# Small VectorE steps of the norms and of a feed-forward layer written as scalar_tensor_tensor in a two-layer hybrid transformer kernel

## The chip, the cores and the metric

The kernel runs on one core of a Trainium2 chip. The metric is the device time of one execution in microseconds (us). Of the kernel before there are three runs: 2148.95, 2151.29 and 2156.46 us, median 2151.29 us. One more execution, 2155.31 us long, was taken with the hardware profiler; all views of the profile below are of that one.

## The reference

The input `x` has 4 sequences of 512 rows and 256 columns, in float32. Eight sublayers follow each other, each on a layer-normalised copy of `x` that is added back:

```python
x = x + mla(layernorm(x))            # low-rank-key attention, 16 heads
x = x + ffn(layernorm(x))            # the feed-forward layer of this change
x = x + cosine_attention(layernorm(x))
x = x + ffn(layernorm(x))            # the same weights again
x = x + gated_linear_attention(layernorm(x))
x = x + workspace(layernorm(x))      # 16 slots a sequence, two rounds
x = x + lora_attention(layernorm(x))
x = x + workspace(layernorm(x))
```

The parts that the change touches are the norms and the feed-forward layer (`eps` is 1e-7 in the latter):

```python
def layernorm(x):  m, v = mean(x), var(x);  return (x - m) / sqrt(v + 1e-5)

def ffn(x):
    out = (x @ weight) * scale
    v_norm = maximum(norm(out), eps)                 # one number a row
    out = out * (tanh(v_norm) / (v_norm + eps))
    o_norm = maximum(norm(out), eps)
    return out * minimum(0.99 / o_norm, 1.0)
```

Row norms of the same kind (a value to the power -1/2) occur in all four attention and workspace layers too.

## The kernel before

A sequence is held in SBUF as 4 tiles of 128 rows by 256 columns (`self.x[b]`, shape 128 x 4 x 256). The four sequences are worked through one after another inside each sublayer, and sublayers overlap: the feed-forward layer of a sequence is a Python generator (`ffn_steps`) whose pieces are called from the loops of the attention layer before or after it (the dictionaries `woven` and `extra`).

By time in the profile the stages are roughly: low-rank attention 0 to 615 us, cosine attention 615 to 1345 us, gated linear attention 1345 to 1580 us, workspace 1580 to 1720 us, LoRA attention 1720 to 2030 us, workspace again to the end.

The order of TensorE's instructions is that of the program text (`tc.manual_schedule(engines={PE})`). The order on VectorE, ScalarE and GpSimd is not written out: a planner makes it when the program is built. It plays the program through with its own costs for each instruction and, whenever an engine is free, takes the ready instruction that ranks first. On the chip each engine then runs its list strictly in that order, and an instruction that has to wait holds up all that stand behind it on its engine.

The lines that matter here:

- `rpow` (line 149) computes `(mul*in + eps)^(-1/2)`. VectorE makes `a = in*mul + eps` (L154, one `tensor_scalar`), ScalarE makes `exp(-0.5*ln(a))` (L155, L156), and VectorE refines it by one Newton step: `t = a*out` (L157, `tensor_tensor`), `t = t*(-0.5)*out` (L158) and `out = (t+1.5)*out` (L160, or L163 into a wide tile), the last two as `scalar_tensor_tensor`. It is called by `moments` for a layer norm (128 x 4 values, mul 1.0, eps 1e-5), by `ffn_steps` (128 x 4, mul 1.0, eps 0.0), by the entry of the workspace layer (128 x 16, mul 1.0, eps 1e-6), and elsewhere with other `mul`: by the query norms of cosine attention (tile `crn`, 128 x 512, in from PSUM), its keys (`crk`), the low-rank keys (`kvrs`) and three norms inside the workspace (`ws_rms`, `ws_ms`, `ws_r`).
- `rpow_aside` is the same on GpSimd and is not touched.
- `ffn_steps` (line 481): after the matmul, `fy = py*scale` (L497, VectorE), four squares with row sums on ScalarE (L500), and then a chain of small steps on 128 x 4 values: a floor (L503), `rpow`, `n*ss` (L505), a floor (L507), tanh on ScalarE (L509) with a change of ScalarE's function table before it and one after it (L510, recorded as L170), `v+eps` (L511), a reciprocal (L512), products and a floor (L513 to L515), a reciprocal (L516), `min(0.99*n, 1)` (L517), a product (L518), and four updates of `x` (L520, already `scalar_tensor_tensor`, 128 x 256).
- GpSimd's larger instructions are the additions of exponentials in cosine attention (L687, 128 x 1024), the scaling of probabilities in low-rank attention (L402), products in gated linear attention (L893, L930 to L933), masks (L1541), rope sums (L1476, L1477) and memsets (L1405 to L1415).

Of the kernel before, what the change touches and what calls it, by code (L numbers as in the profile page):

```python
# [13 lines left out]
ALU = mybir.AluOpType  # L14
# [6 lines left out]
NI = T // P  # L21
# [4 lines left out]
class Model:  # L26
# [122 lines left out]
    def rpow(self, out, in_, mul, eps, tmp, wide=None):  # L149


        nc = self.nc
        a, t = tmp
        nc.vector.tensor_scalar(a, in_, mul, eps, op0=ALU.mult, op1=ALU.add)  # L154
        nc.scalar.activation(out, a, AF.Ln)  # L155
        nc.scalar.activation(out, out, AF.Exp, scale=-0.5)  # L156
        nc.vector.tensor_tensor(t, a, out, op=ALU.mult)  # L157
        nc.vector.scalar_tensor_tensor(t, t, -0.5, out, op0=ALU.mult, op1=ALU.mult)  # L158
        if wide is None:
            nc.vector.scalar_tensor_tensor(out, t, 1.5, out, op0=ALU.add, op1=ALU.mult)  # L160
        else:
            t, r = (v.unsqueeze(len(v.shape)).to_broadcast(wide.shape) for v in (t, out))
            nc.vector.scalar_tensor_tensor(wide, t, 1.5, r, op0=ALU.add, op1=ALU.mult)  # L163

    def tmps(self):
        return [self.small.tile([P, NI], F32, name=f"rp{k}", tag=f"rp{k}") for k in range(2)]
# [314 lines left out]
    def ffn_steps(self, b, pause=True):  # L481
        nc = self.nc
        w, s = self.ffn_w, self.ffn_s
        eps = 1e-7
        xn, xt = self.norm_tiles()
        self.layernorm(xn, self.x[b])
        p2 = self.norm
        if pause:
            yield
        self.turned(xn, xt)  # L490
        yield
        py = self.two().rearrange("p a (i d) -> p (a i) d", d=D)
        for i in range(NI):
            self.mm(py[:, i, :], [(xt[:, c, i * P : (i + 1) * P], w[:, c, :]) for c in range(NC)])
        y = p2.tile([P, NI, D], F32, name="fy", tag="fy")
        ss = self.small.tile([P, NI], F32, name="f_ss", tag="f_ss")
        nc.vector.tensor_tensor(y, py, s.unsqueeze(1).to_broadcast([P, NI, D]), op=ALU.mult)  # L497
        for i in range(NI):
            sq = p2.tile([P, D], F32, name="fsq", tag="fsq")
            nc.scalar.activation(sq, y[:, i, :], AF.Square, accum_out=ss[:, i : i + 1])  # L500

        n = self.small.tile([P, NI], F32, name="f_n", tag="f_n")
        nc.vector.tensor_scalar_max(ss, ss, 1e-30)  # L503
        self.rpow(n, ss, 1.0, 0.0, self.tmps())
        nc.vector.tensor_tensor(n, n, ss, op=ALU.mult)  # L505
        v = self.small.tile([P, NI], F32, name="f_v", tag="f_v")
        nc.vector.tensor_scalar_max(v, n, eps)  # L507
        f = self.small.tile([P, NI], F32, name="f_f", tag="f_f")
        nc.scalar.activation(f, v, AF.Tanh)  # L509
        self.logs()  # L510
        nc.vector.tensor_scalar_add(v, v, eps)  # L511
        nc.vector.reciprocal(v, v)  # L512
        nc.vector.tensor_tensor(f, f, v, op=ALU.mult)  # L513
        nc.vector.tensor_tensor(n, n, f, op=ALU.mult)
        nc.vector.tensor_scalar_max(n, n, eps)  # L515
        nc.vector.reciprocal(n, n)  # L516
        nc.vector.tensor_scalar(n, n, 0.99, 1.0, op0=ALU.mult, op1=ALU.min)  # L517
        nc.vector.tensor_tensor(f, f, n, op=ALU.mult)  # L518
        for i in range(NI):
            nc.vector.scalar_tensor_tensor(  # L520
                self.x[b][:, i, :], y[:, i, :], f[:, i : i + 1], self.x[b][:, i, :], op0=ALU.mult, op1=ALU.add
            )
        yield
# [1314 lines left out]
```

## Time and profile before

| what | value |
|---|---|
| median of three runs | 2151.29 us |
| the profiled execution, whole | 2155.31 us |
| its span, first to last instruction | 2153.5 us |
| VectorE busy | 1268.0 us, 3185 instructions |
| GpSimd busy | 577.8 us, 530 instructions |
| TensorE's mean granted clock | 0.971 |

The 1.8 us between the whole execution and its span lie ahead of the first instruction and behind the last. "Busy" counts an instruction from its recorded start to its recorded end, so that an instruction that has started, but is held up, counts as busy. The names in a line of the profile are those of the tiles, `out<-in`; `DVE` is VectorE, `PE` TensorE, `ACT` ScalarE, `POOL` GpSimd, and `L503` is line 503 of the kernel before.

### The profile page before, as it was taken

To read this page: it belongs to the slowest core of one execution; us is meant where nothing else is said; L and a number is where in the kernel's file an instruction comes from. 1 tells how busy PE (TensorE), PEld (TensorE's weight loads), DVE (VectorE), ACT (ScalarE), POOL (GpSimd) and SP (SyncE) were. 2 spreads that over 40 slices of the span, in tenths; PEclk is the share of its full clock that TensorE was granted. 3 is DMA by queue.
4 is the path that set the end of the run, shared out by engine and by line. 5 is a ranking of instruction groups with operands and counts; after the bars stand their busy time and mean duration, and the time that the engine had idled before them with its cause. 6 is when DMAs were issued, how large, how long until landed. Compare 5 with 4: busy or idle time off the path is not lost.

```text
span 2153.5 us, 25620 instructions
## 1 busy us (share of the span) xinstructions
PE 1988.9 (92%) x9414; PEld 1062.3 (49%) x9414; DVE 1268.0 (59%) x3185; ACT 761.1 (35%) x1696; POOL 577.8 (27%) x530
## 2 busy tenths in 40 slices
PE   7999999999899999999999999988988989899886
PEld 4546555564454454544454454523355644444454
DVE  5565655656446434653664454398955766656545
ACT  2433443434323222322232223234224334334542
POOL 2433333433302212212212221156720122212100
PEclk9999999999999999999999999988899999999898
DMA  5020000000000000000000000010000000000001
GB/s 177 1 91 1 1 1 1 1 1 1 20 1 0 0 1 0 0 1 0 0 1 0 1 0 0 1 46 0 1 25 1 1 1 1 1 1 1 1 1 40
DMA packets 19837, 22.87 MB, mean 11 GB/s; under 512 B 4832, under 2 KB 17664, under 8 KB 19328
## 3 DMA queue, kind: packets, MB, share of 16 engines
q1 hardware_dynamic: 19712, 21.24, 3.0%
q8 instruction: 74, 1.21, 0.2%
q14 instruction: 51, 0.42, 0.1%
HBM read 19.14 MB, written 2.10 MB: 10 GB/s over the span
## 4 chain that ended last, share of the span: by engine, by line
PE 62%; DVE 16%; issue 11%; ACT 6%; POOL 4%; DMA 1%; SPq 0%; POOLq 0%; DVEq 0%; ACTq 0%
PE ps_two L238 26%; PE ps_acc L238 11%; PE ps_two L390 5%; PE ps_acc L429 3%; PE ps_two L1508 3%; DVE ps_two L256 3%; PE ps_two L417 2%; POOL e L687 2%; PE ps_two L1551 2%; DVE gs L888 2%; PE ps_acc L1249 1%; PE ps_two L654 1%; DVE ln_st L178 1%; ACT prob L397 1%; PE ps_acc L645 1%
## 5 line engine op out<-in xcount | busy, mean ns | idle before, releaser
L687 POOL TENSOR_TENSOR e<-e 128x1024 f32<-128x1024 f32 x64 | 150.7, 2355 | 619.4 <-ACT e L679 592.2
L256 DVE CUSTOM_DVE_ANT_0 ps_two<-ps_two,mask 128x256 f32<-128x256 f32 (+3 forms) x512 | 249.7, 503 | 74.3 <-PE ps_two L390 40.7
L679 ACT ACTIVATE e<-ps_two 128x1024 f32<-128x1024 f32 x128 | 130.8, 1023 | 346.8 <-PE ps_two L238 346.6
L238 PE MATMUL ps_acc<-e,cv 128*128 128x512 f32 x512 | 234.9, 601 | 1.4 <-DVE cot L685 0.9
L402 POOL TENSOR_TENSOR prob<-prob,psum_row 128x256 f32<-128x256 f32 (+3 forms) x128 | 159.7, 1255 | 284.6 <-DVE psum_row L401 278.4
L238 PE MATMUL ps_two<-cq,ckt 128*128 128x512 f32 x512 | 230.5, 593 | 3.0 <-DVE cq L656 3.0
L397 ACT ACTIVATE prob<-ps_two,nmax 128x128 f32<-128x128 f32 (+3 forms) x256 | 132.5, 526 | 148.6 <-DVE nmax L256 139.4
L238 PEld LDWEIGHTS ps_acc<-e,cv 128*128 128x128 f32 x512 | 93.5, 190 | 138.3 <-issue 116.0
L238 PEld LDWEIGHTS ps_two<-cq,ckt 128*128 128x128 f32 x512 | 96.6, 190 | 116.9 <-issue 114.8
L238 PE MATMUL ps_two<-own_xt,s 128*128 128x512 f32 x200 | 108.7, 675 | 13.9 <-DVE prt L129 11.1
L238 PE MATMUL ps_two<-own_xt,s16a 128*128 128x512 f32 x256 | 114.9, 592 | 0.1
L238 PE MATMUL ps_two<-s16b,cot 128*128 128x256 f32 x512 | 113.1, 379 | 0.0
L1540 ACT ACTIVATE lo_ex<-ps_two 128x1024 f32<-128x1024 f32 (+3 forms) x128 | 85.3, 704 | 72.8 <-PE ps_two L1508 67.5
L390 PE MATMUL ps_two<-kvt,qx 64*128 64x256 f32 (+3 forms) x512 | 103.6, 481 | 6.1 <-ACT qx L378 2.4
L417 PEld LDWEIGHTS ps_two<-ident,prob 128*128 128x128 f32 x640 | 71.0, 142 | 74.6 <-issue 48.5
L417 PE MATMUL ps_two<-ident,prob 128*128 128x128 f32 x640 | 94.6, 279 | 14.0 <-ACT qx L378 4.5
L238 PEld LDWEIGHTS ps_two<-s16b,cot 128*128 128x128 f32 x512 | 97.3, 190 | 20.1 <-issue 7.7
L1541 POOL TENSOR_SCALAR_AFFINE_SELECT lo_ex<-lo_ex 128x256 f32<-128x256 f32 x128 | 51.7, 408 | 193.5 <-ACT lo_ex L1540 192.3
L688 DVE TENSOR_TENSOR es<-e 128x512 f32<-128x512 f32 x64 | 43.9, 687 | 95.0 <-POOL e L687 93.9
L390 PE MATMUL ps_two<-kpe,qy 64*128 64x256 f32 (+3 forms) x512 | 90.5, 430 | 0.9 <-POOL qy L324 0.9
L1508 PE MATMUL ps_two<-lo_qm,lo_t 32*128 32x128 f32 (+3 forms) x512 | 76.2, 475 | 11.6 <-ACT lo_ex L1540 5.3
L429 PE MATMUL ps_acc<-prt,kv 128*64 128x256 f32 (+3 forms) x512 | 79.0, 452 | 2.7 <-DVE prt L129 2.7
(429 smaller groups left out, 3400.9 us busy)
## 6 DMA issues: line engine op xcount, KB each, us to landing
x<-in_x SPq DMA_DIRECT2D x4, 512.0 KB, 7.7
s16b<-in_mla_wo SPq DMA_DIRECT2D x1, 2048.0 KB, 18.6
s16a<-in_cos_wq SPq DMA_DIRECT2D x1, 2048.0 KB, 9.3
s16b<-in_cos_wo SPq DMA_DIRECT2D x1, 2048.0 KB, 8.6
out_x<-x SPq DMA_DIRECT2D x4, 512.0 KB, 2.9
s16a<-in_mla_wqn SPq DMA_DIRECT2D x1, 1536.0 KB, 13.6
s<-in_mla_wqa SPq DMA_DIRECT2D x1, 1024.0 KB, 10.4
s4a<-in_mla_wkb SPq DMA_DIRECT2D x1, 512.0 KB, 7.4
```

The costliest lines, as they stand in the source:

```text
L238: self.nc.tensor.matmul(out, lhsT=l, rhs=r, start=k == 0, stop=k == n - 1)
L256: self.nc.vector.tensor_tensor_reduce(out=sc[:, :n], in0=sc[:, :n], in1=self.mask[:, T - n :], scale=-1.0, scalar=3.0e38, op0=ALU.add, op1 ...
L390: nc.tensor.matmul(sc[:, k, :n], lhsT=q[r, rows], rhs=key[r, :n], start=first, stop=not first)
L397: nc.scalar.activation(pr[:, k, :n], sc[:, k, :n], AF.Exp, bias=nm[:, k : k + 1], scale=-1.0, accum_out=sm[:, k : k + 1],)
L402: nc.gpsimd.tensor_tensor(pr[:, :, :n], pr[:, :, :n], sm.unsqueeze(2).to_broadcast([P, 2, n]), op=ALU.mult)
L417: nc.tensor.transpose(pt[:, k, keys], pr[:, k, keys], self.ident)
L429: nc.tensor.matmul(po[k * R : (k + 1) * R, j * P :], lhsT=s.kv[:, j, 0, :], rhs=prt[:, k, j, j * P :], start=j == 0, stop=j == NI - 1,)
L679: nc.scalar.activation(t.e[:, pair * 2 : pair * 2 + 2, :], sc, AF.Exp)
L687: nc.gpsimd.tensor_tensor(e2, t.e[:, 0:2, :], t.e[:, 2:4, :], op=ALU.add)
L1508: nc.tensor.matmul(scs[k // 2][:, k % 2, : keys], lhsT=left[r, rows], rhs=right[r], start=True, stop=True)
L1540: nc.scalar.activation(ex[:, hs, :], sc[:, :, :n], AF.Exp, scale=0.25)
L1541: nc.gpsimd.affine_select(out=ex[:, hs, :P], in_=ex[:, hs, :P], compare_op=ALU.is_ge, fill=0.0, base=0, pattern=[[0, 2], [1, P]], channel_ ...
```

## The change

All edits are on VectorE and are of form; the values computed are the same up to rounding. In `rpow`, `in*mul+eps` is written as `max(in+eps, in)` by one `scalar_tensor_tensor` that reads the same tile twice, where `mul` is 1.0 and `eps` not negative; other calls keep `tensor_scalar`. The product `a*out` becomes `(a*1.0)*out`, also one `scalar_tensor_tensor`, in every call. In `ffn_steps` the floors, the addition of `eps`, the products and the final minimum are treated likewise; the minimum takes its 1.0 from the tile `ones` in place of a constant. The number of instructions stays the same.

```diff
         a, t = tmp
-        nc.vector.tensor_scalar(a, in_, mul, eps, op0=ALU.mult, op1=ALU.add)
+        if mul == 1.0 and eps >= 0.0:
+            nc.vector.scalar_tensor_tensor(a, in_, eps, in_, op0=ALU.add, op1=ALU.max)
+        else:
+            nc.vector.tensor_scalar(a, in_, mul, eps, op0=ALU.mult, op1=ALU.add)
         nc.scalar.activation(out, a, AF.Ln)
         nc.scalar.activation(out, out, AF.Exp, scale=-0.5)
-        nc.vector.tensor_tensor(t, a, out, op=ALU.mult)
+        self.product(t, a, out)
...
+    def product(self, out, a, b):
+        self.nc.vector.scalar_tensor_tensor(out, a, 1.0, b, op0=ALU.mult, op1=ALU.mult)
...
-        nc.vector.tensor_scalar_max(ss, ss, 1e-30)
+        floor = lambda out, t, low: nc.vector.scalar_tensor_tensor(out, t, low, t, op0=ALU.max, op1=ALU.max)
+        floor(ss, ss, 1e-30)
         self.rpow(n, ss, 1.0, 0.0, self.tmps())
-        nc.vector.tensor_tensor(n, n, ss, op=ALU.mult)
+        self.product(n, n, ss)
...
-        nc.vector.tensor_scalar_max(v, n, eps)
+        floor(v, n, eps)
...
-        nc.vector.tensor_scalar_add(v, v, eps)
+        nc.vector.scalar_tensor_tensor(v, v, eps, v, op0=ALU.add, op1=ALU.max)
         nc.vector.reciprocal(v, v)
-        nc.vector.tensor_tensor(f, f, v, op=ALU.mult)
-        nc.vector.tensor_tensor(n, n, f, op=ALU.mult)
-        nc.vector.tensor_scalar_max(n, n, eps)
+        self.product(f, f, v)
+        self.product(n, n, f)
+        floor(n, n, eps)
         nc.vector.reciprocal(n, n)
-        nc.vector.tensor_scalar(n, n, 0.99, 1.0, op0=ALU.mult, op1=ALU.min)
-        nc.vector.tensor_tensor(f, f, n, op=ALU.mult)
+        nc.vector.scalar_tensor_tensor(n, n, 0.99, self.ones[:, :NI], op0=ALU.mult, op1=ALU.min)
+        self.product(f, f, n)
```

## The prediction

> **What bounds the kernel.** I read the page first: the busy times and the chain that ended last.
>
> ```profile
> span 2153.5 us, 25620 instructions
> ...
> PE 1988.9 (92%) x9414; PEld 1062.3 (49%) x9414; DVE 1268.0 (59%) x3185; ACT 761.1 (35%) x1696; POOL 577.8 (27%) x530
> ...
> PE 62%; DVE 16%; issue 11%; ACT 6%; POOL 4%; DMA 1%; SPq 0%; POOLq 0%; DVEq 0%; ACTq 0%
> ```
>
> TensorE is the bound, busy 92% of the span. A change on VectorE is worth only what it takes from the 165 us in which TensorE idles (2153.5 - 1988.9). So the second view is busy time by stage:
>
> ```profile
> 615.00:1345.00 730.00, 722.63 (x2324) 354.47 (x2323) 380.13 (x634) 213.09 (x290) 155.50 (x66) 1.00 0.00 0
> 1345.00:1480.00 135.00, 118.47 (x393) 52.99 (x392) 91.92 (x138) 47.63 (x76) 54.24 (x40) 0.90 0.07 19
> ```
>
> After the stretch come busy times of TensorE, weight loads, VectorE, ScalarE and GpSimd. In cosine attention (615 to 1345) TensorE idles 7.4 us of 730: VectorE's delays are covered there. In gated linear attention (to 1480) it idles 16.5 us of 135: there a late VectorE shows.
>
> The third view is of the touched lines: shortest, median and longest duration in ns.
>
> ```profile
> L154 DVE TENSOR_SCALAR rp<-ln_mv x36: 144/168/2391, 6.6 to 2034.3; 128x4 f32<-128x4 f32 x36
> L157 DVE TENSOR_TENSOR rp<-rp,ln_rstd x36: 132/162/2321, 7.3 to 2036.4; 128x4 f32<-128x4 f32 x36
> L157 DVE TENSOR_TENSOR crp<-crp,crn x16: 691/810/928, 620.2 to 1323.7; 128x512 f32<-128x512 f32 x16
> L158 DVE SCALAR_TENSOR_TENSOR rp<-rp,ln_rstd x36: 134/161/165, 7.5 to 2036.6; 128x4 f32<-128x4 f32 x36
> L160 DVE SCALAR_TENSOR_TENSOR ln_rstd<-rp,ln_rstd x36: 132/162/720, 7.7 to 2036.8; 128x4 f32<-128x4 f32 x36
> ```
>
> A step on 128 x 4 values takes some 165 ns in each of the three forms, but a few `tensor_scalar` and `tensor_tensor` take over 2 us. The timeline shows why, and whether the new form escapes (the last five lines are of a later place, GpSimd's first):
>
> ```profile
> 659.85 2.35 POOL L687 TENSOR_TENSOR e<-e 128x1024 f32<-128x1024 f32 x1 [9.35 <-ACT e L679]
> 660.20 2.02 DVE L503 TENSOR_SCALAR f_ss<-f_ss 128x4 f32<-128x4 f32 x1 [3.85 <-ACT fsq L500]
> ...
> 1716.92 0.73 POOL L1476 TENSOR_TENSOR lo_wide<-lo_r,lo_r 128x256 f32<-128x256 f32 x1 [26.19 <-DVE rp L158]
> 1717.61 0.72 POOL L1477 TENSOR_TENSOR lo_wide<-lo_r,lo_r 128x256 f32<-128x256 f32 x1
> ...
> 1716.94 0.72 DVE L160 SCALAR_TENSOR_TENSOR ln_rstd<-rp,ln_rstd 128x4 f32<-128x4 f32 x1
> 1717.58 0.15 DVE L158 SCALAR_TENSOR_TENSOR rp<-rp,ln_rstd 128x4 f32<-128x4 f32 x1
> 1717.77 0.58 DVE L160 SCALAR_TENSOR_TENSOR ln_rstd<-rp,ln_rstd 128x4 f32<-128x4 f32 x1
> ```
>
> L503 starts while GpSimd runs L687 and ends with it (659.85 + 2.35 = 662.20; 660.20 + 2.02 = 662.22): it is held until GpSimd is done. L160 is a `scalar_tensor_tensor` on two SBUF tiles, the new form, and is held in the same way: 0.72 us up to the end of L1476, 0.58 us up to the end of L1477. Other rows say the same: L158 at 1467.29 takes 0.29 under L931, L160 at 1419.32 takes 0.58 under L1017, and L520 (normal 477 ns) takes up to 2585. The new form is no way around GpSimd. L158's spotless row only means that L157 ahead of it has taken the wait already.
>
> **The change, part by part.** 216 executed instructions change form: L154 in 46 (36 layer norms, 8 feed-forward passes, 2 workspace entries), L157 in all 98, and nine steps of `ffn_steps` in 8 passes. None is added or moved in the text, and no DMA or cross-engine dependency changes.
>
> *Own duration.* 86 are `tensor_scalar` now (46 + 5 x 8). Unheld they take 168 ns by L154's median, the new form 161 by L158's: 86 x -7 ns = -0.6 us. The small products go from 162 to 161, nothing. The 16 products on 128 x 512 are 691 ns at the shortest in L157, and L158 on the same tiles has 678 to 692: at most 16 x -13 ns = -0.2 us. Few of these lie where TensorE waits; bounds -0.8 and 0, I take -0.3.
>
> *Waits for GpSimd.* In the touched instructions I sum what exceeds 170 ns (691 for 128 x 512), leaving out excesses up to 40 ns: 29.2 us in 40 instructions, of which L157 has 12.0, L503 7.4, L154 2.9, L507 2.1, L511 2.0, L518 1.5, L513 1.3. For the products, two SBUF tiles before and after, the L160 rows settle it: 0 gained. For the 86 former `tensor_scalar`, the new form reads one tile twice, which no row of the trace shows. If such a step waited no more, the next product on the same data would run into the same GpSimd instruction: L503 at 660.20 would end at 660.4, ScalarE's logarithm and exponential (0.20 each) would end near 660.9, and L157 would be held until 662.2 anyway. What could be gained so is bounded by TensorE's gaps: 0.45 us behind L503 (once; the three later L503 waits have none behind them) and 2.06 at 1469.00 (L507 holds 2.23; behind its tanh stands the copy `gv` for which TensorE idles 5.34). Bounds 0 and -2.5; I take 0, by the nearest row, L160.
>
> *Order of arrival.* L158 at 1717.58 slipped in where one GpSimd instruction ended and the next began, while L154 at 1416.01 had to wait through two. A new form in L154's place may slip in; L157 is then held to the end of L893 at 1418.38, and the chain, which now ends with L160 at 1419.90, ends some 0.9 earlier. Bounds 0 and -0.9; I take -0.4. Under a memset, L154 at 1585.11 took 0.39 us, and L158 at 1587.84 took 0.16: -0.2 us, before which VectorE next idles for ScalarE.
>
> The Trainium skill (SBUF — State Buffer, "Who interferes with whom") says that a VectorE instruction with two SBUF inputs contends with a GpSimd instruction that reads SBUF, whatever its name, and not with one that only writes. It speaks against the change, and agrees with L160 under L1476 and L158 under a memset. A former `tensor_scalar` that reads its tile twice has two SBUF inputs, so by this rule the second part is 0 too, and the sum stays as it is; no run here shows that case.
>
> *Sum.* -0.3 + 0 - 0.4 - 0.2 = -0.9 us, bounds -4.4 and 0. Against the profiled execution that is 2155.3 - 0.9 = 2154.4; this one lies 4.0 above the median of the runs, so against the median: 2151.3 - 0.9 = 2150.4. No wait is added. What gives the cover in cosine attention is TensorE's own backlog; without it, the 12 us of L157 and 7.4 of L503 would be open, but they are so before and after alike.
>
> **What can't be read from the trace** is the planner. It orders VectorE, ScalarE and GpSimd by its own price for each form. If the new forms have other prices there, a ready instruction may overtake another, and since engines run in order, this can open or close gaps that have nothing to do with the form. A place where order costs now:
>
> ```profile
> 232.50 0.17 DVE L503 TENSOR_SCALAR f_ss<-f_ss 128x4 f32<-128x4 f32 x1 [2.20 <-ACT fsq L500]
> 233.46 0.68 DVE L129 COPY prt<-ps_two 128x512 f32<-128x512 f32 x1
> 234.20 1.16 PE L238 MATMUL ps_two<-own_xt,s 128*128 128x512 f32 x1 [2.01 <-DVE prt L129]
> ```
>
> L503 stands ahead of a copy that frees a PSUM tile; VectorE idles 2.20 us for ScalarE's squares, and TensorE 2.01. It recurs at 373.83 and 515.49.
>
> **Rivals.**
> 1. *The wait goes after all.* For it: most waits sit on the touched forms. Against it: L160, L520, L158. All held time is 29.2 us, but on TensorE's path lie 2.2 (L154 at 1416.01), 2.06 + 0.27 (L507, and L157 at 1465.80) and 0.45: 5.0, so 2146.3. The waits of L157 in the low-rank stage (three of 1.26 us) have no TensorE gap of that size behind them.
> 2. *Order moves, for the better.* The three gaps of 2.01 and three of 1.00 behind the same copy (122.71, 269.93, 411.57) close: -9.0, so 2142.3; with 5 us of the two gaps of 5.40 and 5.34 in gated linear attention, 2137.3.
> 3. *Order moves, for the worse*: another step of a feed-forward chain, L511 say, which now idles 1.28 us for tanh, lands ahead of a copy that frees PSUM. Price 2.01 us each, by the row above. It decides from four such gaps (8.0 us, 2159.3); one in each of the 8 passes gives 16.1, 2167.4. For it: the feed-forward chain has five hand-overs between VectorE and ScalarE, and TensorE has little slack outside cosine attention. Against it: the number and dependencies of instructions are unchanged.
>
> **How the numbers follow.** About 0.3%, 6.5 us, is what a measurement of this kernel can tell from no change (its own runs spread by 7.5 us). Forecast, nothing but the small sum: 0.48, 2150.4. Rival 1: 0.07, nearly all of it within 0.3% (5.0 is under 6.5; 0.02 beyond). Rival 2: 0.18, faster. Rival 3: 0.27, slower; I put it above rival 2 because the gaps that order could close are fewer than the places where it could open one. Faster 0.18 + 0.02 = 0.20, same 0.48 + 0.05 = 0.53, slower 0.27. Range from rival 2's far end, 2137, to rival 3's, 2167; the forecast alone would have 2144 to 2158.
>
> **What would show it.** Right: L503, L157, L507 and L511 in the new form still have rows of 1 to 2.3 us that end with a GpSimd instruction; VectorE's busy time stays within 2 us of 1268.0; the gaps at 232, 374 and 515 stay. Rival 1: these rows shrink to 0.17 and VectorE's busy time falls by some 29 us. Rivals 2 and 3: the sequence of lines around L129, L503 and L511 differs, and TensorE's idle time by stage moves with it. I am wrong above all if small differences in the planner's prices reshuffle whole stages.

## The result and the profile after

The changed kernel takes 2159.64 us (median of 22 runs, 2151.40 to 2164.83) against 2150.22 us for the kernel before (22 runs, 2144.47 to 2157.68): 1.0035 of before, 95% interval 1.0025 to 1.0045, some 7.5 us slower (the quotient of the two medians, 1.0044, lies inside the interval). All ratios here leave out four executions that ran at a mean clock of 0.605 to 0.833 and took 2380 to 3098 us. The profiled execution took 2164.1 us.

Lines of `after` are numbered up to 7 higher: L154 is L155 (new form), L157 is the body of `product`, L169, L503 and L507 are L509 (`floor`), L1107, L1108, L1116 are L1114, L1115, L1123. All other kernels below keep the numbers of before.

The page of the profile after:

```profile
span 2162.3 us, 25621 instructions
...
PE 1996.6 (92%) x9414; PEld 1065.9 (49%) x9414; DVE 1269.4 (59%) x3185; ACT 760.4 (35%) x1696; POOL 576.7 (27%) x530
...
PE 62%; DVE 17%; issue 11%; ACT 5%; POOL 4%; DMA 1%; SPq 0%; POOLq 0%; DVEq 0%; ACTq 0%
```

VectorE is as busy as before (1268.0). TensorE is busy 7.7 us longer with the same 9414 instructions: its clock was lower, not its waiting longer (165.7 us idle, 164.6 before). The touched lines (ns, shortest, median, longest) and two places of the timeline that the prediction named:

```profile
L155 DVE SCALAR_TENSOR_TENSOR rp<-ln_mv x36: 127/156/2368, 6.6 to 2035.7; 128x4 f32<-128x4 f32 x36
...
L509 DVE SCALAR_TENSOR_TENSOR f_ss<-f_ss x8: 163/1087/2017, 233.0 to 1463.8; 128x4 f32<-128x4 f32 x8
L509 DVE SCALAR_TENSOR_TENSOR f_v<-f_n x8: 151/157/2219, 237.2 to 1468.4; 128x4 f32<-128x4 f32 x8
```

```profile
233.99 0.68 DVE L129 COPY prt<-ps_two 128x512 f32<-128x512 f32 x1
234.73 1.69 PE L244 MATMUL ps_two<-own_xt,s 128*128 128x512 f32 x3 [2.01 <-DVE prt L129]
...
660.97 2.35 POOL L694 TENSOR_TENSOR e<-e 128x1024 f32<-128x1024 f32 x1 [9.35 <-ACT e L686]
661.32 2.02 DVE L509 SCALAR_TENSOR_TENSOR f_ss<-f_ss 128x4 f32<-128x4 f32 x1 [3.85 <-ACT fsq L506]
```

The held rows are still there: a `scalar_tensor_tensor` that reads one tile twice waits for GpSimd too (660.97 + 2.35 = 663.32, 661.32 + 2.02 = 663.34). The gap of 2.01 us behind the copy `prt` is there as well.

TensorE runs the same instructions in the same order in both kernels, so the two profiles can be laid side by side instruction by instruction. How much later after is at the end of each stretch than at its start, and how much of that is TensorE idle:

```
stretch, before's time (us)   later by   of it idle
   0 to 1565                    -2.3        -3.2
1565 to 1615                    +3.5        +1.8
1615 to 2018                    +0.2        +1.4
2018 to 2068                    +4.1        +1.3
2068 to 2118                    +3.3         0.0
2118 to the end                  0.0         0.0
```

So 7.4 of the 8.8 us between the two spans arise behind 2018 us, in the second workspace layer, most of it without idle time. The 3.5 us from 1565 on lie where after's layernorm is held by memsets (last section), and the stretch ahead of it makes up for a part. There the lists differ. Between the two programs, the lists of TensorE, GpSimd and SyncE are equal; VectorE's differs at five places and ScalarE's at four. One of them is the entry of the second workspace layer (c and d are the third and fourth sequence):

```
ScalarE  before  L155, L156, L1107 c, L1107 d
         after   L1107 c, L155, L156, L1107 d
VectorE  before  L157, L158, L163, L1108 c, L1108 d
         after   L1108 c, L157, L158, L1108 d, L163
```

L1107 and L1108 copy transposed input out of PSUM; L154 to L163 are the norm chain whose end, `ws_norm`, TensorE needs next (L1116). The timeline of before, and then of after, with lines left out:

```profile
2038.34 0.22 ACT L155 ACTIVATE ws_ms<-ws_rp 128x16 f32<-128x16 f32 x1
2038.70 1.14 ACT L1107 COPY ws_xt<-ps_two 128x512 f32<-128x512 f32 x2
2038.83 0.18 DVE L157 TENSOR_TENSOR ws_rp<-ws_rp,ws_ms 128x16 f32<-128x16 f32 x1 [0.53 <-ACT ws_ms L156]
...
2039.25 0.69 DVE L163 SCALAR_TENSOR_TENSOR ws_norm<-ws_rp,ws_ms 128x512 f32<-128x512 f32 x1
2039.86 1.28 DVE L1108 COPY ws_xt<-ps_two 128x512 f32<-128x512 f32 x2
2040.00 1.16 PE L1116 MATMUL ps_acc<-ident,ws_norm 128*128 128x128 f32 x8 [0.78 <-DVE ws_norm L163]
```

```profile
2039.50 0.17 DVE L155 SCALAR_TENSOR_TENSOR ws_rp<-ws_ms 128x16 f32<-128x16 f32 x1
2040.30 0.59 ACT L1114 COPY ws_xt<-ps_two 128x512 f32<-128x512 f32 x1 [0.62 <-PE ps_two L1111]
2040.78 0.22 ACT L158 ACTIVATE ws_ms<-ws_rp 128x16 f32<-128x16 f32 x1
2040.92 0.69 DVE L1115 COPY ws_xt<-ps_two 128x512 f32<-128x512 f32 x1 [1.24 <-ACT ws_xt L1114]
2041.53 0.17 DVE L169 SCALAR_TENSOR_TENSOR ws_rp<-ws_rp,ws_ms 128x16 f32<-128x16 f32 x1
...
2042.54 0.69 DVE L1115 COPY ws_xt<-ps_two 128x512 f32<-128x512 f32 x1 [0.64 <-ACT ws_xt L1114]
2043.15 0.68 DVE L166 SCALAR_TENSOR_TENSOR ws_norm<-ws_rp,ws_ms 128x512 f32<-128x512 f32 x1
2043.88 0.94 PE L1123 MATMUL ps_acc<-ident,ws_norm 128*128 128x128 f32 x6 [2.00 <-DVE ws_norm L166]
```

Before, ScalarE starts its logarithm 0.04 us after L154 ends (2038.13 + 0.17). After, L155 is done at 2039.67, but ScalarE stands with a copy that waits for transposes, and starts the logarithm at 2040.78; VectorE waits 1.24 and 0.64 us with copies that stand ahead of steps of the chain. TensorE idles 2.00 instead of 0.78 us.

The other 6 us are clock. The same stretch of after by windows of 3.41 us (busy times of TensorE, weight loads, VectorE, ScalarE and GpSimd, then TensorE's granted clock), and the second round of the layer:

```profile
2034.85:2038.26 3.41, 1.49 (x8) 0.78 (x7) 2.56 (x13) 2.24 (x6) 0.00 (x0) 1.00 0.00 0
2038.26:2041.67 3.41, 3.41 (x17) 3.22 (x15) 2.06 (x9) 2.01 (x5) 0.00 (x0) 0.50 0.00 0
2041.67:2045.09 3.42, 1.42 (x14) 1.09 (x16) 1.49 (x4) 0.60 (x2) 0.00 (x0) 1.00 0.00 0
2045.09:2048.50 3.41, 3.41 (x17) 0.48 (x14) 0.00 (x0) 0.57 (x1) 0.00 (x0) 0.50 0.00 0
2109.94:2113.35 3.41, 1.11 (x9) 0.50 (x12) 1.81 (x7) 1.59 (x4) 0.00 (x0) 1.00 0.02 5
2113.35:2116.77 3.42, 3.42 (x32) 1.36 (x32) 0.00 (x0) 0.00 (x0) 0.00 (x0) 0.50 0.00 0
```

Each of the three windows here in which TensorE was idle 1.9 to 2.3 us is followed by one at half clock, which by its length costs up to 1.7 us (half of 3.41, an estimate). All half-clock stretches of a profile begin on one grid of 3.413 us (within 0.01 us), and at the start the grid lies elsewhere in each execution. The second round has the same gaps in before (1.37 us at 2095.37, 1.62 at 2104.82, 0.68 at 2106.12), yet no half-clock window; there the grid cuts the gaps elsewhere, and the last two apart:

```profile
2101.36:2104.77 3.41, 1.83 (x5) 0.53 (x3) 3.17 (x9) 1.00 (x3) 0.00 (x0) 1.00 0.00 0
2104.77:2108.19 3.42, 2.56 (x36) 1.35 (x36) 0.07 (x1) 0.59 (x1) 0.00 (x0) 1.00 0.02 5
```

Three theories came out of this. *Order*: the moved list entries cost the time, the workspace entry above all. *Form*: the new instructions cost it after all. *Clock*: half-clock windows are the larger part of it, wherever the first delay comes from.

### The profile page after: what moved, and what is told of

Same layout as the page of the kernel before. It is cut to its first block, busy times and chain, and to the rows that moved or that the text cites. A ratio compares the mean times of both kernels' runs of the same rounds, so it can differ in the third digit from the quotient of the medians.

```text
span 2162.3 us, 25621 instructions
## 1 busy us (share of the span) xinstructions
PE 1996.6 (92%) x9414; PEld 1065.9 (49%) x9414; DVE 1269.4 (59%) x3185; ACT 760.4 (35%) x1696; POOL 576.7 (27%) x530
## 4 chain that ended last, share of the span: by engine, by line
PE 62%; DVE 17%; issue 11%; ACT 5%; POOL 4%; DMA 1%; SPq 0%; POOLq 0%; DVEq 0%; ACTq 0%
PE ps_two L244 25%; PE ps_acc L244 10%; PE ps_two L396 5%; PE ps_acc L435 3%; PE ps_two L1515 3%; DVE ps_two L262 3%; PE ps_two L423 2%; POOL e L694 2%; PE ps_two L1558 2%; DVE gs L895 2%; PE ps_acc L1256 1%; DVE ln_st L184 1%; PE ps_two L661 1%; ACT prob L403 1%; DVE ps_st L892 1%
```

## The experiments

The order of a list was held by edges between neighbours that set the order and add no wait. With before's own order written out in this way, the program is instruction for instruction that of before.

```diff
     with tile.TileContext(nc, schedule_with_timeline_sim=True) as tc:
         emit(tc, aps)
+        traced = {i.name: i for i in nc.cur_bb.bb.instructions}
+        order_only = mybir.DependencyInfo(mybir.DependencyClass.NoSync, mybir.DependencyReason.DATA)
+        for first, second in ORDER:      # neighbours in VectorE's and in ScalarE's list
+            if first in traced and second in traced:
+                tc.add_manual_dep(traced[second], first, order_only, reason="order")
```

### Form and order apart

Forms only: all edits of the change, with `ORDER` from the program of before.

> All new forms, with VectorE's and ScalarE's lists held in the order of before. Order theory (the time comes from the few steps that stand elsewhere in the lists): 1.000 of before, 2149 to 2152 us. Form theory (a scalar_tensor_tensor step itself costs more than what it replaces): 1.0035, 2157 to 2159 us. Clock theory (any small shift of arrivals moves the half-clock windows, whatever its cause): somewhere between, with PE busy and not idle time off by several us.

Measured: 2154.90 us, before 2155.22 in the same session; 0.9997 (0.9983 to 1.0012).

Order only: no edit of the change, with `ORDER` from the program of after.

> The old forms, with VectorE's and ScalarE's lists held in the order of after. Order theory: 1.0035 of before, 2157 to 2159 us. Form theory: 1.000, 2149 to 2152 us. Clock theory: between, and the two effects of this run and of the forms alone need not add up to the whole.

Measured: 2160.60 us, 1.0022 (1.0009 to 1.0036). Against the forms alone, on the same chip, the means differ by 6.0 us (95%: 4.2 to 7.8). The form theory falls: the loss is in the order. The timeline of the order alone has after's gap ahead of the norms' matmuls:

```profile
2039.48 1.16 PE L1116 MATMUL ps_acc<-ident,ws_norm 128*128 128x128 f32 x8 [2.00 <-DVE ws_norm L163]
```

Its busy times and clock in the second round:

```profile
2090.00:2125.00 35.00, 28.51 (x160) 16.27 (x159) 14.03 (x42) 11.37 (x45) 0.00 (x0) 0.90 0.00 1
```

A clock of 0.90 over 35 us is two half-clock windows (2 x 3.41 x 0.5 / 35 = 0.10); the forms alone have 1.00 there.

### Which of the moves

The workspace entry alone (the two lists of the table above in after's order, all else before):

> The old forms and the order of before, but for the second workspace entry (about 2040 us), where the PSUM copies L1107 and L1108 stand ahead of steps of the norm chain as in after. Workspace theory: 1.0025 to 1.0035 of before, 2155.5 to 2158 us (the aligned profiles lose 4.1 us there and 3.4 us in half-clock windows soon behind). Theory that the other moves cost it: 1.000, 2149 to 2152 us.

Measured: 2155.41 us, 1.0004 (0.9988 to 1.0021): less than expected, and compatible with no effect at all. The others without it (cosine attention, LoRA attention, a layernorm):

> The old forms, with all other moves of after (cosine attention, LoRA attention, the layernorm ahead of the workspace) and the second workspace entry as in before. Workspace theory: 1.000 to 1.0007 of before, 2149 to 2152 us. Theory that the other moves cost it: 1.003 and over, 2156 us or more.

Measured: 2153.33 us, 0.9990 (0.9977 to 1.0004). The other moves show no cost of their own. The two halves add up to less than the whole (1.0022), so the entry was tried from the other side: the changed kernel, with that entry alone put back.

> The changed kernel, with its order, but for the second workspace entry, where the copies L1107 and L1108 go back behind the norm chain. Workspace theory: 0.999 to 1.0007 of before, TensorE idles 0.8 us and not 2.0 us ahead of the norms' matmuls, and no half-clock window between 2090 and 2120 us. Theory that it takes all moves together, or the forms: 1.002 to 1.0035, as after.

Measured: 2154.51 us, 1.0002 (0.9985 to 1.0019). The loss is gone. In the timeline TensorE goes from the transposes into the norms' matmuls without a gap (the line has no idle time in brackets):

```profile
2037.26 1.06 PE L1116 MATMUL ps_acc<-ident,ws_norm 128*128 128x128 f32 x8
```

And the clock of the second round is whole:

```profile
2090.00:2125.00 35.00, 28.52 (x217) 18.94 (x216) 16.15 (x50) 9.24 (x32) 1.24 (x2) 1.00 0.00 1
```

The entry alone and the changed kernel were then measured once more on one chip:

> Once more the old forms and order but for the second workspace entry, since the first measurement (1.0004, from 0.9988 to 1.0021) held both theories. Workspace theory: 1.001 to 1.003 pooled, with a part of the executions at 2151 to 2156 us and a mean clock of 0.973 to 0.976 (no late half-clock windows) and a part at 2159 to 2161 us and 0.970 (both). Theory that the other moves are needed for the cost: 0.999 to 1.0005 again.

> The changed kernel's instructions and order once more, as the partner on the same chip for the next runs. Every theory: 1.0025 to 1.0045 of before. Clock theory: its profile has two half-clock windows between 2090 and 2125 us, as in the three profiles with the new order of the second workspace entry, and unlike the six with the old one.

Measured: the entry alone 2158.76 us, 1.0019 (1.0007 to 1.0031); the changed kernel 2159.35 us, 1.0026 (1.0013 to 1.0039). So the entry alone does cost time, in the mean of its two measurements 1.0012, or 2.5 us. Its executions fall into two groups, as expected: of 23, 9 have a mean clock of 0.970 or less and take 2160.3 us on average, 14 have more and take 2154.5. Of before, 8 of 65 in the same two sessions have 0.970 or less. Both profiles of the entry alone are of the first group; the second has none.

The same program twice gave the measure of such differences:

> The instructions and the order of before, unchanged, as a measure of what two equal programs show. Every theory: 1.000 of before within 0.0015. Clock theory: its profile has no half-clock windows between 2090 and 2120 us, like the profiles with the old order of the second workspace entry so far (3 of 3), and unlike those with the new order (3 of 3 have two there).

Measured: 2151.44 us, 1.0000 (0.9984 to 1.0017). No half-clock window lies between 2090 and 2120 us. Yet its profiled execution took 2164.32 us, 9 us more than the one of before; the reason for 5.4 of them stands in the last section.

### Gap or clock

If idle time costs more through the clock than by itself, matmuls that do nothing should help where TensorE waits anyway (`keep(n)` issues n matmuls whose result is not used). First with the order of after and the old forms, at both workspace entries:

```diff
                 if first:
-                    norms()
+                    self.keep(2, pn); norms()
...
-                self.keep(3)
+                self.keep(3 if first else 4)
```

> The order of after with the old forms, and filler matmuls on TensorE at both workspace entries: two ahead of the norms' matmuls, where it idles 1.1 to 1.3 us in the first entry and 2.0 us in the second, and a fourth beside the three there are where it idles 1.62 us in the second round. A filler is about 0.86 us. If only the longer wait costs: no gain, 1.002 to 1.003 of before (2160 to 2162 us; some 0.6 us are added at the first entry). If half-clock windows behind the idle time cost the larger part: these windows go from 2035 to 2050 and from 2095 to 2120 us, and 3.5 to 5 us of the loss come back, 1.000 to 1.001.

Measured: 2157.33 us, 1.0014 (1.0001 to 1.0028). The order alone had 1.0022 in another session, so this by itself decides little. Then in the changed kernel, at the second entry alone (`woven` is empty there), beside the changed kernel on the same chip:

```diff
-                    norms()
+                    (woven or self.keep(2, pn)); norms()
...
-                self.keep(3)
+                self.keep(3 if first or woven else 4)
```

> The changed kernel in its order, with three filler matmuls on TensorE in the second workspace entry alone: two ahead of the norms' matmuls, where it idles 2.0 us, a fourth beside three in the second round, where it idles 1.62 us. If the longer wait alone costs: as after, 1.0025 to 1.0045 of before. If half-clock windows behind the idle time cost the larger part: none between 2090 and 2125 us, and 3 to 5 us come back, 1.0005 to 1.002 of before.

Measured: 2155.46 us, 1.0013 (1.0001 to 1.0026). The mean lies 4.9 us below the changed kernel's (95%: 2.0 to 7.7), with three filler matmuls more (six in the profile, which records each as two), and the mean granted clock is 0.9727 instead of 0.9704. In the timeline the norms still come late, but TensorE is busy for 1.7 of the 2.0 us:

```profile
2039.63 1.88 PE L244 MATMUL ps_acc<-mask,ident 128*128 128x512 f32 x4
2041.80 1.16 PE L1116 MATMUL ps_acc<-ident,ws_norm 128*128 128x128 f32 x8 [0.28 <-DVE ws_norm L163]
```

And the window behind it, half clock in after (2045.09), is at full clock:

```profile
2042.97:2046.38 3.41, 3.41 (x20) 1.20 (x21) 1.38 (x2) 0.59 (x1) 0.00 (x0) 1.00 0.00 0
```

Over all profiles: with the new order of the entry and no filler, two half-clock windows lie between 2090 and 2125 us in 5 of 5; with filler in 0 of 2; with the old order in 1 of 7. The one is the last kernel below, so the old order is no guarantee. What separates the 12 profiles without filler is where the second round lies on the grid. Its first gap, the 1.37 us ahead of L1104, begins 2.70 to 3.07 us behind a grid line in the six without half-clock windows there. In the six with them it begins 3.14 to 3.30 us behind one, or, with the entry alone, 0.60 and 0.62 us. In before and then in after:

```profile
2095.37 1.94 PE L1104 MATMUL ps_acc<-ident,ws_xf 128*128 128x128 f32 x8 [1.37 <-DVE ws_xf L1328]
2100.85 1.94 PE L1111 MATMUL ps_acc<-ident,ws_xf 128*128 128x128 f32 x8 [1.37 <-DVE ws_xf L1335]
```

That place is not chance alone. Early on, at the first matmul L390 (27.47 us in before), the 14 profiles are spread over the grid, 0.66 to 3.14 us behind a line; at the first L238 ahead of the second entry (2028.57 in before) all lie 1.89 to 2.36 us behind one. Each half-clock window shifts what follows against the grid, which could draw the executions together; no run was made on that.

### A better order

Six copies L129 of low-rank attention go ahead of what VectorE waits with: ahead of L503 where TensorE idles 2.01 us, ahead of one L256 where it idles 1.00 us. Forms and all other order are those of before.

> The old forms and the order of before, but for six copies L129 in latent attention that go ahead of what VectorE waits with: ahead of the feed-forward step L503 at three places, ahead of one masked maximum L256 at three. If a place in VectorE's list is worth what TensorE idles behind it: three gaps of 2.01 us shrink to 0.2, three of 1.00 us to 0.3, and two half-clock windows behind the large ones go (1.7 us each), 0.9950 to 0.9965 of before. If the waits only move to the next matmul that hangs on L256: 0.999 to 1.000.

Measured: 2145.98 us, 0.9976 (0.9957 to 0.9996). Better, by half to two thirds of what was expected. In the timeline the copy comes 2.5 us earlier and its gap closes, while a new one opens behind the next copy, on ScalarE:

```profile
230.91 0.69 DVE L129 COPY prt<-ps_two 128x512 f32<-128x512 f32 x1 [1.28 <-PE ps_two L417]
231.66 1.98 PE L238 MATMUL ps_two<-own_xt,s 128*128 128x512 f32 x4
...
239.92 1.09 PE L218 MATMUL ps_two<-ident,xn 128*128 128x128 f32 x8 [2.33 <-ACT prt L133]
```

Last, all of the change's forms with this order, and L198 in the new form too:

```diff
-                    nc.vector.tensor_scalar(
-                        dst[:, i, :], src[:, i, :], mv[:, i, 0:1], rstd[:, i : i + 1],
+                    nc.vector.scalar_tensor_tensor(
+                        dst[:, i, :], src[:, i, :], mv[:, i, 0:1], rstd[:, i : i + 1].to_broadcast([P, D]),
```

> All new forms in the order of before, with the six copies L129 moved ahead as in the run of that edit alone, and the layernorm's L198 on VectorE as scalar_tensor_tensor too (four instructions, at the workspace entries). If a tensor_scalar of one source waits there for a row of GpSimd memsets and a scalar_tensor_tensor doesn't: L154 and L198 at the first entry stay under 0.5 us each (0.38 to 5.70 and 0.41 to 3.02 us so far), executions over 2158 us vanish, 0.9960 to 0.9975 of before. If it does: a 3 to 6 us step remains in one execution of four or so, as in the run with the copies alone (0.9976).

Measured: 2147.45 us, 0.9967 (0.9950 to 0.9983), faster than both kernels. L154 and L198 stay under 0.5 us at the first entry, as the last section shows. Two of its 7 counted executions lie over 2151 us with a clock of 0.970 or less, so the clock still scatters its time.

## Why the prediction was wrong

*The forms: right as far as the measurement tells.* The prediction summed them to -0.9 us, bounds -4.4 and 0. Forms alone measure 0.9997 (0.9983 to 1.0012), which is -0.6 us with some 3 us to either side, too wide to tell -0.9 from 0. The rows that it named as the mark are there: L509 with 2.02 us at 661.32, ending with GpSimd; VectorE's busy time 1.4 us from 1268.0; the gaps of 2.01 us. Rival 1, that the wait goes, is out for the steps under GpSimd's `tensor_tensor`.

*Two terms of the sum.* Of "order of arrival" (-0.4) nothing came: L155 at the very place, 1416.55 in after, still takes 2.37 us (L154 at 1416.01 in before: 2.39). The memset term (-0.2) was the right mechanism at the wrong size. L154 at 1585.11, priced by its 0.39 us, took 0.38 to 0.39 us in five of 8 profiles of the old form, and 1.28, 5.69 and 5.70 in the others.

*The step that failed* is "Forecast, nothing but the small sum", given 0.48: it let the lists of VectorE and ScalarE stand. They moved at nine places, and one of these, the entry of the second workspace layer, decides. Of the argument against rival 3, "the number and dependencies of instructions are unchanged", the runs show that it proves nothing: the same number and dependencies with another order cost 1.0022.

*Rival 3* had the direction and about the time (2159.3; measured 2159.6), but by another mechanism. It had a feed-forward step ahead of a copy that frees PSUM, at 2.01 us each and from four places on. The runs have two copies ahead of a norm chain, at one place, and 1.2 us more idle time there. The price was wrong because it took a gap for what it lasts: in the profiles beside each other the entry costs 4.1 us and the second round 3.3, of which 1.3 are idle time and the rest is half clock. The chain of waits and the idle time by stage, on which the prediction rested, can't show that; the clock at 0.971 on before's table could have warned of it: 0.029 of 2153.5 us is 62 us of clock not granted, all but some 6 of them ahead of TensorE's last instruction.

*Rival 2* did not happen by itself, but its six gaps were real: moving the copies by hand brought some 5 us (0.9976) of the 9.0 that it priced, and a new gap opened behind the next copy.

*What stays open.* Undone in the changed kernel, the entry is worth 6 us (1.0030, the mean of two, to 1.0002); alone it costs 2.5. The traces show where the two part. From the first L238 ahead of the entry to L1152 behind it (2028.57 to 2046.65 in before) the profiles of the old order without filler take 18.1 to 18.3 us, the entry alone 19.3, and the changed kernel and the order alone 22.2. In these three the wait of 2.00 us begins 0.18 to 0.26 us behind a grid line, lies in one window, and half clock follows; with the entry alone it begins 2.67 and 2.70 us behind one, the next line cuts it, and none follows:

```profile
2042.36 1.16 PE L1116 MATMUL ps_acc<-ident,ws_norm 128*128 128x128 f32 x8 [2.00 <-DVE ws_norm L163]
```

This is read from five profiles; no run moved the grid alone.

## What to carry to other kernels

A change of form that leaves every duration alone can still move a planned order, so compare the instruction lists first, and hold the old order to measure the form. Where TensorE's clock drops behind idle time, price a gap with the clock: a wait 1.2 us longer cost some 6 us here, and filler matmuls in the wait brought 4.9 us back without removing it. Copies that nothing waits for yet belong behind the chain that the next matmul needs.

## What the runs showed of the hardware

The clock: in the second workspace layer of the changed kernel half-clock windows of 3.41 us follow windows with 1.9 to 2.3 us of TensorE idle time in one or two gaps, none longer than 2.00 us. The bound is not sharp: 1.35 us of idle time ahead of 2103.1 in after was enough, 1.58 us from 2101.36 in before was not. Elsewhere in before 1.90 us from 626.83 had no half clock behind it and 1.18 us from 2009.23 had. The Trainium skill (TensorE: Matmul & The Clock Gate, "Why this matters for your kernels") warns of idle gaps over some 3 us; by these profiles shorter ones do it, and the measurement decides.

GpSimd's memsets hold a `tensor_scalar` and not a `scalar_tensor_tensor`. In the timeline of the second profile of before's program, L154 started in a row of memsets and ended with it, at 1592.85; TensorE comes out of the first workspace entry 5.4 us later than in the first profile, 3.9 of it idle:

```profile
1587.01 0.52 POOL L1415 MEMSET lo_nm<- 128x512 f32 x1
1587.16 5.69 DVE L154 TENSOR_SCALAR rp<-ln_mv 128x4 f32<-128x4 f32 x1
...
1592.62 0.20 POOL L1411 MEMSET lo_v<- 128x64 f32 x1
```

In the new form it takes 0.16 us among the same memsets, in 6 profiles of 6. In two of these, after among them, the layernorm's L198 ran into the row instead (L204 in after: 3.34 us for two, against 0.41 us each at the second entry, where GpSimd is idle). As `scalar_tensor_tensor`, in the last kernel's timeline, it took 0.87 us for two beside them:

```profile
1576.92 0.16 DVE L154 SCALAR_TENSOR_TENSOR rp<-ln_mv 128x4 f32<-128x4 f32 x1
...
1579.70 0.87 DVE L198 SCALAR_TENSOR_TENSOR ws_xf<-x,ln_mv,ln_rstd 128x256 f32<-128x256 f32 x2
1579.87 0.53 POOL L1415 MEMSET lo_nm<- 128x512 f32 x1
```

So the change does what its form promises at one place, against memsets, and not against GpSimd's instructions that read. The Trainium skill (SBUF — State Buffer, "Who interferes with whom") says both: a `tensor_scalar` can contend with GpSimd in a two-port mode, and a VectorE instruction with two SBUF inputs contends with GpSimd's reads and not with its writes. The rows agree; the mode itself stands in no trace.
